# Block L1 of a four-layer decoder: VectorE's order written out, weights rounded behind the clips, both partial sums on one engine, output tiles spread over the batches

## The chip, the core and the metric

The kernel runs on one core of a Trainium2 chip. The metric is the device time of one execution in microseconds. All times of engines below come from one profiled execution, in microseconds from the start of its span unless marked otherwise.

Engines are called as in the profile: PE is TensorE, PEld its weight loads, DVE VectorE, ACT ScalarE, POOL GpSimd, SP the queue that issues most DMAs.

## What is computed

Four layers of cross attention and a feed-forward network (FFN) over 8 batches of 100 tokens of 512 numbers, with a context of 361 positions a batch. The change touches layer L1 alone:

```
# attention: 16 heads of 32, keys and values from the context
q, k, v = proj(layernorm(x)), proj(context), proj(context)
scores = clip(q @ k / sqrt(32), -50, 50); masked positions become -50
probs  = softmax(scores); probs = probs / (sum(probs) + 1e-8)
delta  = clip(residual_scale, 0, 0.3) * (probs @ v @ Wo.T + bo)
x      = x + layernorm(delta) * gamma + beta
# FFN with ternary weights (w1 is 2048 x 512, w2 512 x 2048)
weight_quant(w)     = clip(round(w / mean|w|), -1, 1) * mean|w|
activation_quant(y) = round(y * 127 / max|y|) / (127 / max|y|), by token
h = relu(activation_quant(layernorm(x)) @ weight_quant(w1).T)
x = x + activation_quant(h) @ weight_quant(w2).T
```

## The kernel before

The 800 tokens lie in SBUF as seven tiles of 128 tokens (the last has 32). L1's attention goes batch by batch. Its functions, with the names that appear in the profile:

- `kv_pieces(b)` makes the keys and values of a batch: four key blocks, each four matmul pairs of TensorE and a copy out of PSUM with bias on ScalarE (`kT`, line 1321), and three value blocks, copied out by VectorE (`va`, line 1329). They are handed out in pieces (`k[0]` to `k[3]`, `v[0]` to `v[2]`), to be put between other work of TensorE.
- `weigh(b, c)` handles chunk c of the context positions (128, 128 and 105 of them): 32 small matmuls give the scores of 16 heads (the last eight use the fourth key block), VectorE clips them in two halves (line 1465), ScalarE takes the Exp of each half (line 1467, tile `pT`).
- Between chunks the three `pT` of a batch are added up, tile `added`: the sum of the first two on GpSimd (line 1473), the third added by VectorE (line 1475).
- `gather(b)` sums over positions with a matmul by ones (`l`), multiplies the weights by the values, and scales by the reciprocal (`rl`, lines 1500 to 1504).
- `Ternary` prepares w1 and w2, four blocks of 128 x 2048 each, through two load buffers `v`: `add_up` takes absolute sums on ScalarE (line 1596), `quantise` scales, clips and rounds in two steps on VectorE (lines 1609 and 1610) and a third on ScalarE (line 1611). `park` writes w2's rounded blocks to DRAM. These steps are `fillers`, a list of 18; one is taken in each of the 18 stages (b = 0 to 5, c = 0 to 2).
- `OutputAndFFN` holds the output projection by tile: `product` (matmul), `scaled` (scale, bias, statistics and a Sqrt), `added` (norm, sum into x, statistics of the new x and a Sqrt), then the FFN by tile: `quantise` (norm and rounding of a tile), `turn_y`, `widen`, `round_h`, `turn_h`, `narrow`.

TensorE's order is the order of the program in this part. `held(...)` does the same for an instruction of another engine; those not held are put in place by a scheduler. In `before`, the steps of `Ternary.quantise` and GpSimd's sum are not held. Work waits for its buffers: TensorE's results have four buffers of one PSUM bank (`ps1`) and two of two banks (`ps2`; a `weigh` takes both).

In `before` each stage of the first six batches runs `weigh`, then the pieces and `gather` of the batch before, and last its filler:

```
weigh(b, c)
...                       # pieces of keys and values, gather(b - 1)
if fillers:
    fillers.pop(0)()
```

Batch 6 and 7 follow written out. The output tiles 0 to 3 stand in batch 6, two ahead of its last chunk and two behind it. In the FFN loop (`run`) tile i + 4's `product` and `scaled` stand ahead of `narrow(i - 1)`, its `added` behind it.

Of the kernel before, what the change touches and what calls it, by code (L numbers as in the profile page):

```python
# [59 lines left out]
def decoder_kernel(ctx: ExitStack, tc: tile.TileContext, a: dict, out: bass.AP):  # L60
# [1365 lines left out]
    def clipped_attention(ctxT, begun, st, fillers, begin_ffn):  # L1426

        root = HR  # L1430
        wq, wk, wv, wo, rs, bqk, bv, msc, mbi, kst, kvp, kv = begun
        res = st.enter_context(tc.tile_pool(name="a1", bufs=1))
        qT = project_q(res, wq, bqk[:, 0, :], held=True)
        hst = st.enter_context(ExitStack())
        hp = hst.enter_context(tc.tile_pool(name="a1h", bufs=2))
        beta = hp.tile([128, 4, KD * LQ], F32, name="pT", bufs=4)[:, 0:2, :].rearrange("p g q -> p (g q)")[:, :D]
        nc.sync.dma_start(out=beta, in_=a["a1_beta"].partition_broadcast(128))
        add_row_to_x(beta)
        ffn = begin_ffn(wq, wo, rs)
        ffn.qT = qT  # L1440

        weights = {}
        added = {}

        def weigh(b, c):

            toks = slice(b * LQ, (b + 1) * LQ)
            k0, kn = KCH[c]
            kT = kv[b][0]
            pT = hp.tile([128, 4, KD * LQ], F32, name="pT", bufs=4)  # L1450
            weights.setdefault(b, []).append(pT)
            s = [ps2(), ps2()]
            for j in range(KD):
                for g in range(4):
                    rows = four_heads(g)
                    matmul(
                        s[g // 2][:kn, g % 2, j * LQ : (j + 1) * LQ],
                        lhsT=kT[rows, j, k0 : k0 + kn],
                        rhs=qT[rows, j, toks],
                        start=True,  # L1460
                        stop=True,
                    )
            for i in range(2):
                dst = pT[:kn, 2 * i : 2 * i + 2, :]
                held(nc.vector.tensor_scalar(dst, s[i][:kn, :, : KD * LQ], LIM * root, -LIM * root, ALU.min, ALU.max))  # L1465
                held(
                    nc.scalar.activation(  # L1467
                        dst, dst, AF.Exp, bias=mbi[:kn, b, c : c + 1], scale=msc[:kn, b, c : c + 1]
                    )
                )  # L1470
            if b < NB - 1 and c == 1:
                added[b] = hp.tile([128, 4, KD * LQ], F32, name="added", bufs=1)
                nc.gpsimd.tensor_tensor(added[b], weights[b][0], pT, ALU.add)
            elif b < NB - 1 and c == 2:
                held(nc.vector.tensor_tensor(added[b][:kn], added[b][:kn], pT[:kn], ALU.add))

        def gather(b):

            _, va, _ = kv.pop(b)
            pTs = weights.pop(b)  # L1480
            p, l = ps1(), ps1()
            parts = [(added.pop(b), 128)] if b in added else [(pT, kn) for pT, (_, kn) in zip(pTs, KCH)]
            for i, (pT, kn) in enumerate(parts):
                if i == 2:
                    yield
# [37 lines left out]
        with in_order():  # L1523
            for b in range(NB - 2):
                k, v = pieces(b + 1) if b else (kv[1][2][0::2], kv[1][2][1::2])
                for c in range(3):
                    weigh(b, c)
                    if b == 0:
                        several(*((k[1], k[2]), (v[1], v[2]), (k[3],))[c])
                    elif c == 0:  # L1530
                        several(k[0], k[1])
                        for _ in gather(b - 1):
                            pass
                        several(v[0])
                    elif c == 1:
                        several(v[1], k[2], v[2])
                    else:
                        several(k[3])
                    if fillers:
                        fillers.pop(0)()  # L1540
            assert not fillers
            k, v = pieces(NB - 1)
            weigh(NB - 2, 0)
            several(k[0], k[1])
            for _ in gather(NB - 3):
                pass
            several(k[2])
            weigh(NB - 2, 1)
            several(k[3])
            for t in (0, 1):  # L1550
                ffn.product(t)
                ffn.scaled(t)
            weigh(NB - 2, 2)
            for t in (2, 3):
                ffn.product(t)
                ffn.added(t - 2)
                ffn.scaled(t)
            weigh(NB - 1, 0)
            several(v[0])
            ffn.added(2)  # L1560
            ffn.added(3)
            for _ in gather(NB - 2):
                pass
            several(v[1])
            ffn.quantise(0)
            weigh(NB - 1, 1)
            several(v[2])
            ffn.quantise(1)
            weigh(NB - 1, 2)
            ffn.turn_y(0, nc.vector.tensor_copy)  # L1570
            last = gather(NB - 1)
            next(last)
            ffn.widen(0, (0, 1))
            next(last)
        hst.close()
        kst.close()
        return ffn
# [3 lines left out]
    class Ternary:  # L1581
# [24 lines left out]

        def quantise(self, i, dst):
            w = load_v(self.src[i])
            nc.vector.tensor_scalar(w, w, self.inv, 1.0, ALU.mult, ALU.min)
            nc.vector.tensor_scalar(w, w, -1.0, MAGIC, ALU.max, ALU.add)  # L1610
            nc.scalar.activation(dst, w, AF.Identity, bias=unmagic)  # L1611

        def park(self, i, spare):

# [34 lines left out]
    class OutputAndFFN:  # L1649
# [18 lines left out]
        def scaled(self, t):  # L1668
# [6 lines left out]
                )  # L1675
            )
            self.done[t] = d
            self.statistics(d, *(v[:rows, t, :] for v in self.stats[0:2]))

        def statistics(self, src, mv, rstd):  # L1680
            st = small.tile([128, 6], F32, name="st")[: src.shape[0]]
            held(nc.vector.bn_stats(st, src))
            held(nc.vector.bn_aggr(mv, st))
            held(nc.scalar.activation(rstd, mv[:, 1:2], AF.Sqrt, bias=eps[: src.shape[0]]))

        def added(self, t):

# [3 lines left out]
            held(nc.vector.reciprocal(rstd, rstd))  # L1691
            held(nc.vector.scalar_tensor_tensor(d, d, mv[:, 0:1], self.gamma[:rows, :], ALU.subtract, ALU.mult))
            held(nc.vector.scalar_tensor_tensor(x[:rows, t, :], d, rstd, x[:rows, t, :], ALU.mult, ALU.add))
            self.statistics(x[:, t, :], *(v[:, t, :] for v in self.stats[2:4]))

        def scales(self, amax, step, mean):

# [99 lines left out]
        def run(self, hp):  # L1797

            q2 = self.w2.fetch()
            for i in range(NTT + 1):  # L1800
# [5 lines left out]
                    self.widen(i, (1,))  # L1806
                if i + 1 < NTT:
                    self.turn_y(i + 1)
                if i < NTT:
                    self.round_h(i, hp)  # L1810
                if i + 2 < NTT:
                    self.quantise(i + 2)
                ahead = i + 4 < NTT
                if ahead:
                    self.product(i + 4)
                    self.scaled(i + 4)
                if i:
                    self.narrow(i - 1, q2)
                if ahead:
                    self.added(i + 4)  # L1820

# [900 lines left out]
```

## Time and profile before

| | |
|---|---|
| times of three runs | 1981.69, 1985.65, 1990.58 us |
| median | 1985.65 us |
| the profiled execution | 1981.62 us, its span 1979.8 us |
| mean granted clock of TensorE | 0.978 |
| L1's batches and FFN | from 602 to 909 us of the span |
| TensorE busy in the span | 1868.0 us (94%) |
| VectorE, ScalarE, GpSimd busy | 851.0, 541.7, 273.3 us |

A line of a timeline gives the start, the duration, the engine, the line of the kernel, the operation, the tile written and the tiles read, their shapes, how many instructions were merged, and in brackets how long the engine stood idle before and what released it. f32 matmuls appear as two instructions each. Where two successive instructions overlap in the pipeline, the time from start to start is what one costs.

### The profile page before, as it was taken

The numbers are of one execution on the slowest core, as the hardware profiler recorded it, in microseconds if no ns is written. First come the engines' busy times: TensorE is split into PE (matmuls) and PEld (weight loads), VectorE is DVE, ScalarE is ACT, GpSimd is POOL, SyncE is SP. The second block draws the span as 40 slices with busy tenths as digits, with TensorE's granted clock in tenths as the row PEclk, the third lists the DMA queues.
The fourth block names the chain that finished last, engine by engine and source line by source line (L and its number), as shares of the span: only waits on it lengthen the run. The fifth ranks groups of instructions, "written<-read, shape, count | busy, mean of one in ns | idle before, by whom it ended". The sixth has DMA issues, their size and how long they took to land.

```text
span 1979.8 us, 28538 instructions
## 1 busy us (share of the span) xinstructions
PE 1868.0 (94%) x11992; PEld 1109.6 (56%) x11992; DVE 851.0 (43%) x1577; ACT 541.7 (27%) x1167; POOL 273.3 (14%) x220
## 2 busy tenths in 40 slices
PE   6999999899989989888999998999999999999996
PEld 3676666343355545434555554555445555569994
DVE  4354444445354584884455555111113443432222
ACT  1243323134414453563244443100001111111110
POOL 4200000033033011001000000000001000033553
PEclk8999999999989999899999999999999999999998
DMA  9601000188953260011000001111101000057883
GB/s 272 214 25 33 24 9 22 37 326 248 293 199 102 86 213 22 23 43 53 22 2 1 1 22 43 43 43 43 43 0 59 16 2 1 12 170 231 267 243 73
DMA packets 62957, 177.21 MB, mean 90 GB/s; under 512 B 19079, under 2 KB 27571, under 8 KB 55905
## 3 DMA queue, kind: packets, MB, share of 16 engines
q1 hardware_dynamic: 35234, 134.08, 20.1%
q0 software_dynamic: 22576, 31.96, 6.2%
q10 hardware_dynamic: 5006, 9.22, 1.4%
q8 instruction: 98, 1.61, 0.3%
q14 instruction: 43, 0.34, 0.1%
HBM read 149.25 MB, written 21.65 MB: 86 GB/s over the span
## 4 chain that ended last, share of the span: by engine, by line
PE 60%; DVE 7%; DMA 5%; ACT 5%; issue 2%; POOL 1%; POOLq 0%; SPq 0%; DVEq 0%; ACTq 0%
PE ps L103 57%; PE ps L108 3%; DMA out_x<-o,r_row 3%; ACT sc L1865 1%; DMA v<-in_f_w 1%; ACT pT L1467 1%; DVE va L1329 1%; ACT h L1775 1%; POOL got L1267 1%; DVE sc L1871 1%; ACT hq L1780 1%; DVE amax L1761 1%; DVE pT L1465 1%; DVE nmx L1861 0%; ACT q_f_w L1611 0%
## 5 line engine op out<-in xcount | busy, mean ns | idle before, releaser
L103 PE MATMUL ps<-yT,w 128*128 128x400 f32 x768 | 263.8, 505 | 0.7 <-DVE yT L83 0.7
L103 PE MATMUL ps<-w,ctxT 128*128 128x512 f32 (+1 forms) x576 | 263.1, 600 | 0.0
L103 PE MATMUL ps<-ctxT,w 128*128 128x361 f32 x768 | 251.3, 476 | 0.0
L103 PEld LDWEIGHTS ps<-yT,w 128*128 128x128 f32 x768 | 146.4, 192 | 114.1 <-issue 5.8
L103 PEld LDWEIGHTS ps<-ctxT,w 128*128 128x128 f32 x768 | 142.5, 191 | 90.8 <-issue 16.2
L103 PEld LDWEIGHTS ps<-w,ctxT 128*128 128x128 f32 (+1 forms) x576 | 102.0, 183 | 117.6 <-issue 109.2
L1321 ACT ACTIVATE kT<-ps,bqk 128x361 f32<-128x361 f32 x96 | 53.5, 559 | 213.4 <-PE ps L103 207.7
L103 PE MATMUL ps<-xT,w 128*128 128x152 f32 (+1 forms) x768 | 104.6, 297 | 1.2 <-ACT xT L85 1.2
L103 PEld LDWEIGHTS ps<-xT,w 128*128 128x128 f32 (+1 forms) x768 | 101.1, 184 | 2.5 <-ACT xT L85 1.5
L1329 DVE TENSOR_TENSOR va<-ps,r_a_bv 128x512 f32<-128x512 f32 (+1 forms) x72 | 49.6, 689 | 116.4 <-PE ps L103 116.4
L103 PE MATMUL ps<-w_vo,oc 128*128 128x512 f32 (+1 forms) x224 | 90.5, 598 | 0.0
L952 DVE TENSOR_TENSOR hT<-sg,ps 128x400 f32<-128x400 f32 x36 | 20.6, 571 | 158.3 <-PE ps L103 156.0
L103 PE MATMUL ps<-w,qT 128*128 128x512 f32 (+1 forms) x184 | 83.4, 619 | 5.0 <-DVE qT L2166 4.7
L233 DVE TENSOR_TENSOR x<-x,ps 128x512 f32<-128x512 f32 (+1 forms) x51 | 34.9, 685 | 121.5 <-PE ps L103 121.4
L1865 ACT ACTIVATE sc<-ps,nmx 100x361 f32<-100x361 f32 x128 | 70.2, 561 | 50.0 <-DVE nmx L1861 50.0
L2178 POOL IOTA counts<- 128x2 f32 x2 | 0.2, 134 | 552.3 <-PE ps L103 552.3
L108 PEld LDWEIGHTS ps<-ident,sc 100*128 100x128 f32 (+1 forms) x512 | 52.8, 148 | 41.0 <-issue 26.1
L2491 POOL DMA_INDIRECT out_x<-o,r_row x32 | 59.4, 1856 | 89.1 <-DMA out_x<-o,r_row 34.8
L666 ACT ACTIVATE sc<-sc,nmx 100x128 f32<-100x128 f32 x128 | 49.8, 390 | 79.4 <-DVE nmx L663 78.6
L108 PE MATMUL ps<-ident,sc 100*128 100x100 f32 (+1 forms) x512 | 61.3, 255 | 6.3 <-DVE va L1329 3.9
L1467 ACT ACTIVATE pT<-pT,mbi,msc 128x800 f32<-128x800 f32 (+1 forms) x48 | 47.9, 1045 | 54.0 <-DVE pT L1465 53.4
L2093 DVE TENSOR_SCALAR kp<-ps,mask 128x512 f32<-128x512 f32 (+1 forms) x48 | 33.8, 747 | 65.2 <-PE ps L103 65.2
(399 smaller groups left out, 2831.2 us busy)
## 6 DMA issues: line engine op xcount, KB each, us to landing
w<-in_f_gu SPq DMA_DIRECT2D x32, 704.0 KB, 6.3
wd<-in_f_dn SPq DMA_DIRECT2D x32, 512.0 KB, 6.2
v<-in_f_w SPq DMA_DIRECT2D x16, 1024.0 KB, 5.5
v<-in_f_dn SPq DMA_DIRECT2D x16, 768.0 KB, 7.5
w<-in_a_w SPq DMA_DIRECT2D x11, 1024.0 KB, 4.9
w<-in_f_gu SPq DMA_DIRECT2D x9, 1024.0 KB, 4.8
gu<-in_f_gu SPq DMA_DIRECT2D x8, 1024.0 KB, 16.6
cx<-in_ctxT SPq DMA_DIRECT2D x8, 722.0 KB, 17.9
```

Of the source, the lines that this page charges most:

```text
L103: ins = nc.tensor.matmul(dst, **args)
L108: ins = nc.tensor.transpose(dst, src, unit)
L233: nc.vector.tensor_tensor(x[:rows, t, :], x[:rows, t, :], p[:rows, :], ALU.add)
L666: nc.scalar.activation(sc[:, g, :], sc[:, g, :], AF.Exp, bias=nmx[:, g : g + 1], accum_out=l[:, g : g + 1])
L952: nc.vector.tensor_tensor(dst, sg[:rows, :n], pu[:rows, :n], ALU.mult)
L1267: nc.gpsimd.indirect_dma_start(out=got[t][:rows, i, :], out_offset=None, in_=back, in_offset=bass.IndirectOffsetOnAxis(ap=where_i[:rows, t ...
L1321: ins = nc.scalar.activation(kT[:, m, :], p[:, :LK], AF.Identity, bias=bk[:, m : m + 1])
L1329: ins = nc.vector.tensor_tensor(va[:kn, c, :, 0:HD], p[:kn, :].rearrange("p (h d) -> p h d", d=HD), bv[:kn, :].rearrange("p (h d) -> p h d ...
L1467: nc.scalar.activation(dst, dst, AF.Exp, bias=mbi[:kn, b, c : c + 1], scale=msc[:kn, b, c : c + 1])
L1865: nc.scalar.activation(sc[:, h, :], s[i][:LQ, g, :LK], AF.Exp, bias=nmx[:, g : g + 1], accum_out=l[:, h : h + 1])
L2093: nc.vector.tensor_scalar(kps[b][:kn, c, 2 * i : 2 * i + 2, :, :].rearrange("p g j f -> p g (j f)"), s[i][:kn, :, : KD * F], 0.0, mask[:kn ...
L2491: nc.gpsimd.indirect_dma_start(out=flat, out_offset=bass.IndirectOffsetOnAxis(ap=r_row[:, e, h : h + 1], axis=0), in_=o[:, h, :], in_offse ...
```

## The change

In each stage of the first six batches the filler stands right behind `weigh`, ahead of the pieces, and the three steps of `quantise` are held, so that VectorE's two steps come right behind the clips. The first sum of a batch (`add(b, 1)`) moves from GpSimd to VectorE and stands behind the pieces of chunk 1; the second (`add(b, 2)`) stands behind the clips of the next batch's first chunk. Output tile 0 moves to the end of chunk 1 of the fifth batch (b = 4), tile 1 to that of the sixth (b = 5), with `added(0)`. Tiles 2 and 3 stay in batch 6. The Sqrt of `added` becomes a step of its own, `rooted`, placed later; in the FFN loop `rooted(i + 2)` stands ahead of `round_h(i)` and `added(i + 3)` behind `quantise(i + 2)`.

```diff
-            if b < NB - 1 and c == 1:
+
+        def add(b, c):
+
+            kn = KCH[c][1]
+            if c == 1:
                 added[b] = hp.tile([128, 4, KD * LQ], F32, name="added", bufs=1)
-                nc.gpsimd.tensor_tensor(added[b], weights[b][0], pT, ALU.add)
-            elif b < NB - 1 and c == 2:
-                held(nc.vector.tensor_tensor(added[b][:kn], added[b][:kn], pT[:kn], ALU.add))
+            other = weights[b][0] if c == 1 else added[b]
+            held(nc.vector.tensor_tensor(added[b][:kn], other[:kn], weights[b][c][:kn], ALU.add))
...
                     weigh(b, c)
+                    if b and c == 0:
+                        add(b - 1, 2)
+                    fillers.pop(0)()
...
-                    if fillers:
-                        fillers.pop(0)()
+                    if c == 1:
+                        add(b, 1)
+                        if b == NB - 4:
+                            ffn.product(0)
+                            ffn.scaled(0)
+                        elif b == NB - 3:
+                            ffn.product(1)
+                            ffn.added(0)
+                            ffn.scaled(1)
             weigh(NB - 2, 0)
+            add(NB - 3, 2)
...
-            for t in (0, 1):
-                ffn.product(t)
-                ffn.scaled(t)
+            ffn.product(2)
+            ffn.rooted(0)
+            ffn.added(1)
+            ffn.scaled(2)
+            add(NB - 2, 1)
             weigh(NB - 2, 2)
-            for t in (2, 3):
-                ffn.product(t)
-                ffn.added(t - 2)
-                ffn.scaled(t)
+            ffn.product(3)
+            ffn.rooted(1)
+            ffn.added(2)
+            ffn.scaled(3)
             weigh(NB - 1, 0)
+            add(NB - 2, 2)
+            ffn.quantise(0)
             several(v[0])
-            ffn.added(2)
-            ffn.added(3)
...
-            nc.vector.tensor_scalar(w, w, self.inv, 1.0, ALU.mult, ALU.min)
-            nc.vector.tensor_scalar(w, w, -1.0, MAGIC, ALU.max, ALU.add)
-            nc.scalar.activation(dst, w, AF.Identity, bias=unmagic)
+            held(nc.vector.tensor_scalar(w, w, self.inv, 1.0, ALU.mult, ALU.min))
+            held(nc.vector.tensor_scalar(w, w, -1.0, MAGIC, ALU.max, ALU.add))
+            held(nc.scalar.activation(dst, w, AF.Identity, bias=unmagic))
...
                     self.turn_y(i + 1)
+                if i + 2 < NTT:
+                    self.rooted(i + 2)
                 if i < NTT:
                     self.round_h(i, hp)
                 if i + 2 < NTT:
                     self.quantise(i + 2)
-                ahead = i + 4 < NTT
-                if ahead:
+                if i + 3 < NTT:
+                    self.added(i + 3)
+                if i + 4 < NTT:
                     self.product(i + 4)
                     self.scaled(i + 4)
                 if i:
                     self.narrow(i - 1, q2)
-                if ahead:
-                    self.added(i + 4)
```

More of the change, by code (lines that the diff above doesn't have):

```diff
@@ L1564, in clipped_attention @@
             several(v[1])
-            ffn.quantise(0)
             weigh(NB - 1, 1)
+            ffn.quantise(1)
             several(v[2])
-            ffn.quantise(1)
             weigh(NB - 1, 2)
+            last = gather(NB - 1)
             ffn.turn_y(0, nc.vector.tensor_copy)
-            last = gather(NB - 1)
             next(last)
@@ L1677, in scaled, with statistics @@
             self.done[t] = d
-            self.statistics(d, *(v[:rows, t, :] for v in self.stats[0:2]))
-        def statistics(self, src, mv, rstd):
+            self.statistics(d, self.stats[0][:rows, t, :])
+            self.root(*(v[:rows, t, :] for v in self.stats[0:2]))
+        def statistics(self, src, mv):
             st = small.tile([128, 6], F32, name="st")[: src.shape[0]]
@@ L1683, in statistics, with root, rooted @@
             held(nc.vector.bn_aggr(mv, st))
-            held(nc.scalar.activation(rstd, mv[:, 1:2], AF.Sqrt, bias=eps[: src.shape[0]]))
+        def root(self, mv, std):
+            held(nc.scalar.activation(std, mv[:, 1:2], AF.Sqrt, bias=eps[: mv.shape[0]]))
+        def rooted(self, t):
+            self.root(*(v[:, t, :] for v in self.stats[2:4]))
         def added(self, t):
@@ L1693, in added @@
             held(nc.vector.scalar_tensor_tensor(x[:rows, t, :], d, rstd, x[:rows, t, :], ALU.mult, ALU.add))
-            self.statistics(x[:, t, :], *(v[:, t, :] for v in self.stats[2:4]))
+            self.statistics(x[:, t, :], self.stats[2][:, t, :])
         def scales(self, amax, step, mean):
```

## The prediction, made before the changed kernel was run

> **What bounds the kernel.** I read the page first, then the timelines of TensorE, VectorE and ScalarE from 575 to 910 us, which is L1.
>
> ```profile
> PE 1868.0 (94%) x11992; PEld 1109.6 (56%) x11992; DVE 851.0 (43%) x1577; ACT 541.7 (27%) x1167; POOL 273.3 (14%) x220
> 643.58 1.00 PE L103 MATMUL ps<-qT,kT 32*105 32x100 f32 x32
> 644.51 2.70 PE L103 MATMUL ps<-ctxT,w 128*128 128x361 f32 x8
> 647.14 1.54 PE L103 MATMUL ps<-qT,kT 32*128 32x100 f32 x32
> ...
> 735.65 2.50 PE L103 MATMUL ps<-qT,kT 32*128 32x100 f32 x24 [5.83 <-DVE pT L1465]
> 739.16 0.77 PE L103 MATMUL ps<-qT,kT 32*128 32x100 f32 x8 [1.01 <-ACT kT L1321]
> 739.86 7.16 PE L103 MATMUL ps<-ctxT,w 128*128 128x361 f32 x16
> ...
> 821.80 0.67 PE L103 MATMUL ps<-qT,kT 32*105 32x100 f32 x4 [7.61 <-DVE pT L1465]
> ...
> 872.33 3.63 PE L103 MATMUL ps<-v,hqT 128*128 128x512 bf16 x16 [2.87 <-ACT hqT L1722]
> ```
>
> TensorE is the bound. The change leaves its matmuls as they are, so I count only what PE loses in L1: idle time, and matmuls at a lower clock. Batches are b = 0 to 7, chunks c = 0 to 2.
>
> ```profile
> 643.69 0.69 DVE L1329 TENSOR_TENSOR va<-ps,r_a_bv 105x512 f32<-105x512 f32 x1 [5.17 <-PE ps L103]
> 644.61 1.89 DVE L1465 TENSOR_SCALAR pT<-ps 105x800 f32<-105x800 f32 x2 [0.23 <-PE ps L103]
> 645.70 2.00 ACT L1467 ACTIVATE pT<-pT,mbi,msc 105x800 f32<-105x800 f32 x2 [2.99 <-DVE pT L1465]
> 647.60 0.54 ACT L1321 ACTIVATE kT<-ps,bqk 128x361 f32<-128x361 f32 x1
> 648.05 1.90 ACT L1596 ACTIVATE q_f_w<-v 128x2048 bf16<-128x2048 f32 x1
> 694.09 3.58 POOL L1473 TENSOR_TENSOR added<-pT 128x1600 f32<-128x1600 f32 x1 [25.99 <-ACT pT L1467]
> 694.46 4.30 DVE L1610 TENSOR_SCALAR v<-v 128x2048 f32<-128x2048 f32 x1
> ```
>
> The first five lines are the turn from one batch to the next. PE's scores of c = 2 end at 644.51, the next batch's scores begin at 647.14, and their last eight matmuls need the fourth key block: clip, two Exps, the key's copy, ready at 648.15. PE loses 0.4 (1.54 against 1.15 elsewhere). The last two lines: a rounding of weights that takes 1.22 alone takes 4.30 beside POOL's sum.
>
> **Lost before.** Four such turns, 1.6. At 703.63, 0.9. At 735, where weights' rounding stands before the clips: 5.83 + 1.01 idle and 4.1 of slow matmuls (2.50, 0.70 and 7.09 from start to start, for 0.81, 0.27 and 5.07): 11.0. At 821, where four output tiles stand before the clips: 7.61 + 0.23 and 3.9 slow, likewise: 11.8. The FFN's ten waits (0.38, 1.25, 0.46, 2.87, 0.65, 1.25, 1.17, 0.99, 2.99, 0.25): 12.3. Sum 37.6.
>
> **Part 1: both sums on VectorE.** Seven POOL sums of 3.57 go, and with them the 3.1 that one cost the rounding. Seven of 1.75 (796.37 to 798.12) come. The first sum of a batch now stands after the last value copy and ahead of the clips of c = 2. With 0 at the end of the value matmuls: copy to 0.7, sum to 2.5, clips to 3.4 and 4.35. The scores were ready at 1.0, so the clips are 1.4 late.
>
> **Part 2: the filler right behind the clips, rounding on ScalarE held.** In the instruction order of the changed kernel, ScalarE has the filler of c = 2 between the Exps and the fourth key copy; before it was the other way round. PE waits for that copy. Undisturbed, PE would reach it at 4.3 (scores 0.93, key 2.6, first scores 0.8). Now (0.1 for a hand-over, as 644.51 to 644.61; Exps of 0.95):
> - b = 0, 1: Exps to 5.4, absolute sum 2.0, copy 0.5, PE at 8.0: 3.7 lost each.
> - b = 2, no filler: PE at 6.0: 1.7.
> - b = 3: rounding on VectorE 2.45 (732.15 to 734.61) to 6.8, on ScalarE 6.9 to 8.85, copy, PE at 9.45: 5.1.
> - b = 4 also has an output tile: PE is due at 7.85 (product 3.5). Its scaling and statistics (1.6, from 3.6) push the clips to 7.05, rounding to 9.5, ScalarE to 11.55, PE at 12.15: 4.3.
> - b = 5 adds `added` (2.4): clips to 8.35, rounding to 10.8, PE at 13.45: 5.6.
> Turns: 24.1. In c = 0 of b = 4 and 5 the rounding delays the first key's copy to 8.7 after the scores, and its PSUM buffer is the value matmul's, due at 7.95: 0.8 each, 1.7. In c = 1 the rounding's 2.45 fits the 5.17 that VectorE stood before 643.69. SP's order does not change; a weight block's load is issued behind the rounding two blocks before and lands 5.6 to 7.9 later; two stages take at least 14 us (c = 1 to the next c = 0), of which that rounding uses 5, so no load is late. If one were, VectorE's line would stand still with the clips behind it, as at 735.
>
> **Part 3: output tiles spread.** The 11.8 goes. Left: the turn to b = 7, 1.0; from the third product's end VectorE has scaling 1.6, sum 1.75, clips 1.85, `added` 2.4, scaling 1.6, clips 1.85, sum 1.75 = 12.9, where PE has 10.0 until it needs that sum: 3.0; before the first wide matmul clips and a copy, 1.8. Together 5.8.
> The Sqrt of a tile now goes out with its tile, which needs an Exp table again (1.28, its Exp 0.01 later). In b = 4 the Exps end at 8.8, where ScalarE waits for VectorE until 9.6; the same 0.8 in b = 5. So it costs nothing, and what it exceeds 0.8 by otherwise. The Trainium skill (ScalarE: Activation LUTs, What ACT_TABLE_LOAD costs) gives 2.66 us a switch, which speaks against this part: by it the two turns would be 0.6 longer each and the sum 1.1 higher; the trace shows no such second half.
>
> **Part 4: roots apart from norms.** In the FFN a tile with a product took 12.3 (854.13 to 866.45) though VectorE has 10.7 of work in it; it stood 1.6 for the Sqrt. With the Sqrt issued a turn ahead, PE's own 11.7 is the bound, and the waits of 1.25, 0.46, 2.87, 0.65 and 0.38 go. A Sqrt ahead of the first rounding brings one of 1.2. 12.3 becomes 7.9.
>
> **Clock.** After: 24.1 + 1.7 + 5.8 + 7.9 = 39.5, against 37.6: 1.9 more, before the clock. Three turns leave PE idle 4.1 in one piece (b = 3, 4, 5), two 2.8, one wait 3.0. What a gap costs:
>
> ```profile
> 1223.72 1.37 PE L108 MATMUL ps<-ident,y 128*128 128x128 f32 x8 [3.00 <-DVE y L200]
> 1224.00:1227.00 3.00, 2.91 (x11) 1.50 (x10) 2.00 (x6) 0.96 (x3) 0.00 (x0) 0.71 0.00 0
> 1227.00:1230.00 3.00, 3.00 (x6) 1.20 (x5) 0.34 (x1) 0.00 (x0) 0.00 (x0) 0.72 0.00 0
> 1955.00:1960.00 5.00, 4.65 (x7) 2.03 (x8) 0.57 (x2) 0.00 (x0) 3.60 (x2) 0.66 0.18 17
> 872.00:874.00 2.00, 1.67 (x8) 0.80 (x9) 2.00 (x5) 0.76 (x2) 0.00 (x0) 1.00 0.93 393
> ```
>
> (Columns: stretch, its length, busy time and instructions of the five engines, granted clock, DMA share, GB/s.) After 3.00 idle the clock was 0.71 and 0.72 for six us, 1.7 lost; after 3.76 (ahead of 1955), 0.66, 1.7 lost; after 2.87, nothing; after 5.83, 4.1. So a gap of 4.1 costs 1.7 to 4.1; I take 2.5, as 3.76 is the nearest: 7.5, less the 1.7 of value waits that a slower PE no longer sees. The three shorter ones lie between nothing and 1.7: half, 2.5. Clock: 8.3. The Trainium skill (TensorE: Matmul & The Clock Gate, Part 1) has the clock halved only after a whole free-running window of some 3.4 us idle, by which the gap of 3.00 should have cost nothing; an estimate by it has a fifth of the 4.1 gaps drop, the sum then near 3; the rows decide.
>
> **Sum.** 1.9 + 8.3 = 10.2; my hand-overs of 0.1 are generous by some 1 over L1, so 9 us. The profiled execution took 1981.62 (span 1979.8), and would take 1990.6. The median of the three runs, 1985.65, is 4.0 above it; 1985.65 + 9 is about 1994.
>
> **Rivals.**
> - Clock at every gap: all six drop for as long as at 735 (4.1 each, 24.6 in place of 8.3). For it: the 2.99 at 907.92 was followed by seven slow microseconds. Against it: 872. It decides once more than four gaps cost 3 or more. 1994 + 16 = 2010. Chance 0.10.
> - The turns are cheap: the key's copy isn't what PE waits for, the first scores run late anyway, and a turn costs 1 in place of 3.7 to 5.6. For it: PE lost only 0.4 there. Against it: 739.16, released by exactly this copy. Price: 24.1 becomes 6, and 8.3 of clock goes: 26 less, 1968. Chance 0.10.
> - Losses only change places: the sum of 39.5 is right and the clock stays up, 1985.65 + 2 = 1988. For it: the skipped drop at 872. Chance 0.12.
>
> **How the numbers follow.** The forecast (0.68) spans 1987 to 2003: clock prices at their ends, hand-overs, and the spread of the runs (4 either way). A measurement of this kernel tells apart about 0.5%, 9.9 us, so its centre is just inside. Of its 0.68 I put 0.36 within and 0.32 above; with the rivals: faster 0.10, same 0.48, slower 0.42. The range takes in the third rival and most of the first, and leaves out the second: 1980 to 2008.
>
> **What would show it.** Right: PE's idle at each turn from b = 0 to 5 released by the kT copy, 2.8 (b = 0, 1) and about 4 (b = 3 to 5), with the filler between Exps and copy on ScalarE; no wait over 5 us at 735 or 821; FFN tiles some 11.7 apart; the clock under 0.8 after the 4 us gaps. Wrong: turns under 1 us, VectorE waiting for a weight load, or batches 1 and 2 as long as before (27.2).

## The result and the profile after

| | before | after |
|---|---|---|
| median of 15 runs | 1985.65 us | 1997.91 us |
| lowest, highest | 1978.79, 1990.58 | 1990.66, 2006.97 |
| profiled execution, its span | 1981.62, 1979.8 | 2006.55, 2004.6 |
| L1, from the first scores to the last narrow product | 306.6 | 319.4 |

The ratio after to before is 1.0067, with a 95% interval of 1.0049 to 1.0084: slower by 13.3 us (9.7 to 16.7). The forecast was 1994, in a range of 1980 to 2008. L1's length is read from the two traces: 908.77 - 602.17 and 926.50 - 607.13, so 12.8 longer. The profiled execution of after lies 8.6 above its median and that of before 4.0 below its own, so these two differ by more than the medians do. The other 12 us of their difference lie ahead of L1 (5.0) and behind it, where the change moves nothing; I read L1 alone.

The totals of the profile of after show little: TensorE is busy for 10.0 more than before with the same 11992 matmuls, which is slow matmuls and not more work (in the whole span, so not in L1 alone).

```profile
PE 1878.0 (94%) x11992; PEld 1115.8 (56%) x11992; DVE 859.9 (43%) x1584; ACT 545.5 (27%) x1169; POOL 247.1 (12%) x213
```

TensorE's timeline of after. The lines ending in x8 with a kT in brackets are the last eight score matmuls of a batch's first chunk. The key blocks are the lines of x16.

```profile
629.27 0.77 PE L103 MATMUL ps<-qT,kT 32*128 32x100 f32 x8 [2.56 <-ACT kT L1321]
629.97 8.03 PE L103 MATMUL ps<-ctxT,w 128*128 128x361 f32 x16
...
662.93 0.60 PE L103 MATMUL ps<-qT,kT 32*128 32x100 f32 x8 [2.62 <-ACT kT L1321]
663.46 6.66 PE L103 MATMUL ps<-ctxT,w 128*128 128x361 f32 x16
...
691.52 0.91 PE L103 MATMUL ps<-qT,kT 32*128 32x100 f32 x20 [0.36 <-DVE pT L1465]
693.16 0.48 PE L103 MATMUL ps<-qT,kT 32*128 32x100 f32 x8 [0.73 <-ACT kT L1321]
...
694.18 6.64 PE L103 MATMUL ps<-ctxT,w 128*128 128x361 f32 x16
...
727.17 0.77 PE L103 MATMUL ps<-qT,kT 32*128 32x100 f32 x8 [4.03 <-ACT kT L1321]
727.86 6.88 PE L103 MATMUL ps<-ctxT,w 128*128 128x361 f32 x16
...
763.81 0.76 PE L103 MATMUL ps<-qT,kT 32*128 32x100 f32 x8 [4.07 <-ACT kT L1321]
764.50 7.33 PE L103 MATMUL ps<-ctxT,w 128*128 128x361 f32 x16
...
802.23 0.76 PE L103 MATMUL ps<-qT,kT 32*128 32x100 f32 x8 [4.07 <-ACT kT L1321]
802.92 6.90 PE L103 MATMUL ps<-ctxT,w 128*128 128x361 f32 x16
...
835.30 0.88 PE L103 MATMUL ps<-added,ones 128*32 128x400 f32 x8 [2.77 <-DVE added L1478]
```

All six turns wait for the fourth key copy; both jams of before (TensorE's waits of 5.83 and 7.61 for clips, at 735 and 821) are gone. Taken from the start of the scores of c = 2 to the start of the next key block, less the 4.64 of the matmuls in between (0.93, 2.63 and 1.08), the turns lose 3.9, 3.8, 1.8, 5.4, 4.7 and 6.0: 25.6. In the turn 2 to 3 a product by ones (0.61) is left out. What was not expected stands in the x16 lines: the key block behind every turn is slow, also behind 693.16, where no gap is over 0.73.

ScalarE's timeline in the turn 3 to 4 shows the chain: two Exps, the rounding's third step, and only then the key's copy.

```profile
721.38 2.00 ACT L1467 ACTIVATE pT<-pT,mbi,msc 105x800 f32<-105x800 f32 x2 [6.09 <-DVE pT L1465]
724.67 2.00 ACT L1627 ACTIVATE q_f_w<-v,unmagic 128x2048 bf16<-128x2048 f32 x1 [1.29 <-DVE v L1626]
726.57 0.54 ACT L1321 ACTIVATE kT<-ps,bqk 128x361 f32<-128x361 f32 x1
```

The granted clock (the share of its full speed that TensorE got) over three of the six key blocks of after (stretch, length, busy time of PE, PEld, DVE, ACT and POOL, clock, DMA share, GB/s):

```profile
629.97:638.00 8.03, 8.03 (x24) 4.55 (x24) 3.78 (x4) 4.46 (x5) 0.00 (x0) 0.63 0.53 192
694.18:700.80 6.62, 6.62 (x21) 3.77 (x24) 3.44 (x7) 2.56 (x3) 0.00 (x0) 0.76 0.01 2
764.50:771.80 7.30, 7.30 (x24) 4.13 (x23) 6.04 (x5) 3.03 (x3) 0.00 (x0) 0.69 0.37 139
```

From start to start the six key blocks take 7.96, 6.58, 6.58, 6.81, 7.26 and 6.82, in place of 5.07: 2.9, 1.5, 1.5, 1.7, 2.2 and 1.8 more, 11.6 in all.

### The profile page after: what moved, and what is told of

Same layout as the page of the kernel before. It is cut to its first block, busy times and chain, and to the rows that moved or that the text cites. A ratio compares the mean times of both kernels' runs of the same rounds, so it can differ in the third digit from the quotient of the medians.

```text
span 2004.6 us, 28525 instructions
## 1 busy us (share of the span) xinstructions
PE 1878.0 (94%) x11992; PEld 1115.8 (56%) x11992; DVE 859.9 (43%) x1584; ACT 545.5 (27%) x1169; POOL 247.1 (12%) x213
## 4 chain that ended last, share of the span: by engine, by line
PE 54%; DVE 6%; ACT 4%; DMA 3%; issue 1%; POOL 0%; POOLq 0%; SPq 0%; DVEq 0%; ACTq 0%
PE ps L103 52%; PE ps L108 3%; DMA out_x<-o,r_row 2%; ACT sc L1889 1%; DMA xs<-normal,r_tok 1%; DVE va L1329 1%; DVE pT L1465 1%; DVE sc L1895 1%; DVE nmx L1885 0%; ACT h L1798 0%; DVE added L1478 0%; ACT hq L1803 0%; ACT q_f_w L1627 0%; ACT pT L1467 0%; DVE y L200 0%
## 5 line engine op out<-in xcount | busy, mean ns | idle before, releaser
L103 PE MATMUL ps<-ctxT,w 128*128 128x361 f32 x768 | 260.9, 490 | 0.0
L103 PEld LDWEIGHTS ps<-ctxT,w 128*128 128x128 f32 x768 | 147.6, 198 | 95.6 <-issue 25.2
L233 DVE TENSOR_TENSOR x<-x,ps 128x512 f32<-128x512 f32 (+1 forms) x51 | 34.9, 685 | 120.5 <-PE ps L103 120.3
```

The costliest lines, as they stand in the source:

```text
L103: ins = nc.tensor.matmul(dst, **args)
L233: nc.vector.tensor_tensor(x[:rows, t, :], x[:rows, t, :], p[:rows, :], ALU.add)
```

## The experiments

Theory: ScalarE's order at the turn (filler ahead of the key's copy), with the first sum's delay of the clips, makes TensorE wait, and the waits pull its clock down. Rivals: VectorE's load is the limit; the sum costs nothing; the slow blocks are something else than the clock; and the FFN's or the tiles' gains do not exist. The kernels in one table. Each ratio is to runs of before taken with it; L1 is read as above, from one trace each:

| kernel | median us | ratio to before (95%) | L1 |
|---|---|---|---|
| after | 1997.91 | 1.0067 (1.0049 to 1.0084) | 319.4 |
| key copy ahead of the filler | 1985.60 | 1.0007 (0.9990 to 1.0025) | 305.6 |
| value block in the turn | 1968.12 | 0.9907 (0.9886 to 0.9929) | 284.5 |
| first sum on GpSimd | 1990.31 | 1.0014 (0.9997 to 1.0031) | 309.7 |
| gaps filled | 1989.77 | 1.0014 (0.9993 to 1.0036) | 308.3 |
| before, FFN part | 1978.21 | 0.9956 (0.9938 to 0.9973) | 299.0 |
| before, tiles spread | 1987.33 | 0.9996 (0.9978 to 1.0015) | 306.6 |
| before, FFN part and value block in the turn | 1977.02 | 0.9947 (0.9925 to 0.9970) | 296.8 |
| value block in the turn, more cover | 1961.24 | 0.9865 (0.9843 to 0.9887) | 280.3 |
| the same, first sum on GpSimd | 1956.52 | 0.9861 (0.9834 to 0.9888) | 278.6 |

One more, with the scores four times, had one execution (1993.0) and is read from its trace.

### Key copy ahead of the filler

```diff
-                    fillers.pop(0)()
+                    if c < 2:
+                        fillers.pop(0)()
...
                         several(k[3])
+                    if c == 2:
+                        fillers.pop(0)()
```

> The changed kernel (1997.9 us) with one line moved: in c = 2 the fourth key block is issued ahead of the filler, so that ScalarE copies the key before it does its absolute sum or rounding. Theory A (ScalarE's order decides the turn, the first sum on VectorE adds its 1.4): the six turns lose 1.7, 1.7, 1.7, 1.7, about 0.7 and 2.0 in place of 3.9, 3.8, 1.8, 5.4, 4.7 and 6.0, so 16 us less; no wait for the key's copy above 2. The clock then splits it in two. A1, only gaps of 2.5 us or more pull the clock down: the 11.6 us that the slow key blocks cost go too, and the time is near 1970. A2, the clock falls where some 3.4 us hold nothing but small score matmuls and short gaps, as after the turn 2 to 3 of the changed kernel (gaps of 0.36 and 0.73 only): the key blocks behind most turns stay at 6.5 in place of 5.07, and the time is near 1980. Rival B (the key's copy is late because VectorE is late, not because of the filler): the waits stay at 2.6 and 4.0, the time at 1998.

TensorE's timeline, turns 0 to 1, 1 to 2 and 4 to 5:

```profile
622.30 0.48 PE L103 MATMUL ps<-qT,kT 32*128 32x100 f32 x8 [0.67 <-ACT kT L1321]
622.71 5.13 PE L103 MATMUL ps<-ctxT,w 128*128 128x361 f32 x16
...
650.89 0.48 PE L103 MATMUL ps<-qT,kT 32*128 32x100 f32 x8 [0.73 <-ACT kT L1321]
651.30 6.80 PE L103 MATMUL ps<-ctxT,w 128*128 128x361 f32 x16
...
746.10 0.48 PE L103 MATMUL ps<-qT,kT 32*128 32x100 f32 x8 [2.01 <-ACT kT L1321]
```

The turns lose 1.7, 1.8, 1.8, 1.8, 2.3 and 3.9, together 13.4 (9.5 expected; the last two came higher, with a tile's scaling and a table load ahead of the clips). So ScalarE's order was worth 12.2 of the 25.6, where 16 were expected. Rival B falls. Of the clock A2 holds: five of the six key blocks stay slow, 9.4 us in place of 11.6. The first turn loses 1.74 and its block runs at 5.13, the second loses 1.80 and its block takes 6.80. 12.2 + 2.2 = 14.4; L1 is 13.8 shorter, the median 12.3.

### Value block in the turn

```diff
-                        several(*((k[1], k[2]), (v[1], v[2]), (k[3],))[c])
+                        several(*((k[1], k[2]), (v[1], k[3]), (v[2],))[c])
...
-                        several(v[1], k[2], v[2])
+                        several(v[1], k[2], k[3])
                     else:
-                        several(k[3])
+                        several(v[2])
```

> The changed kernel with two blocks of TensorE swapped in the first six batches: the fourth key block moves into c = 1 and the third value block into c = 2, so that behind the scores of c = 2 stands a block that no score matmul waits for, and the first sum no longer stands behind that value copy. Filler and sums stay where the change put them. Theory A (the turn costs what it does because TensorE waits for the fourth key copy): no wait for a key copy at the turns, 25.6 us of turn losses become under 3, and the stretch without a dense block shrinks to about 1.2 us, so that the 11.6 of slow clock go as well: about 1962, below the kernel before (1985.65). Rival B (VectorE is the bound at the turn: clips, sum, rounding): the waits come back as waits for clips or for a value's PSUM buffer, and the time stays above 1985. Rival C (the clock falls for another reason than what stands at the turn): the waits go, the key blocks stay at 6.6 to 7.9, and the time is near 1974.

TensorE's timeline, the turn 1 to 2 and two places of c = 0:

```profile
645.92 3.68 PE L103 MATMUL ps<-w,ctxT 128*105 128x512 f32 x8
649.53 1.15 PE L103 MATMUL ps<-qT,kT 32*128 32x100 f32 x32
650.61 5.13 PE L103 MATMUL ps<-ctxT,w 128*128 128x361 f32 x16
...
713.48 3.70 PE L103 MATMUL ps<-w,ctxT 128*128 128x512 f32 x8 [0.87 <-ACT kT L1321]
...
745.33 3.70 PE L103 MATMUL ps<-w,ctxT 128*128 128x512 f32 x8 [1.57 <-ACT kT L1321]
```

The turns have no gap, and the six key blocks take 5.11 to 5.14. L1 is 34.9 shorter than in the changed kernel and the median 29.8; expected were 36. Rivals B and C fall: once TensorE has other work at the turn, the filler and the sums where the change put them no longer hold it up there. The swap also takes the first sum from behind the third value copy, so this run does not part the two. The waits of 0.87 and 1.57, which Rival B named, are new but small; they are the value's PSUM buffer of the prediction, discussed below.

### First sum on GpSimd

```diff
-            held(nc.vector.tensor_tensor(added[b][:kn], other[:kn], weights[b][c][:kn], ALU.add))
+            if c == 1:
+                nc.gpsimd.tensor_tensor(added[b], other, weights[b][c], ALU.add)
+            else:
+                held(nc.vector.tensor_tensor(added[b][:kn], other[:kn], weights[b][c][:kn], ALU.add))
```

> The changed kernel with the first sum of each batch (weights of c = 0 plus c = 1) back on GpSimd; everything else as changed. Theory A (on VectorE it delays the clips of c = 2 by 1.4): each turn's wait for the key copy falls by 1.4, to 1.2 in b = 0 and 1, to nothing in b = 2 and to 2.7 in b = 3 to 5; 8 us less, and 1.5 more where the clock stays up after the turn 2 to 3: 1989. If the clock also stays up after the turns whose gap falls to 1.2, 1985. Rival B (the sum fills a hole of VectorE and costs nothing, the filler on ScalarE is all): waits as before this edit, 1998. Rival C (GpSimd's sum slows the roundings beside it from 1.25 to over 4, as at 694.46 of the kernel before): roundings of 4, and the time at 1998 or above.

TensorE's timeline, turns 2 to 3, 3 to 4 and 4 to 5:

```profile
687.17 1.54 PE L103 MATMUL ps<-qT,kT 32*128 32x100 f32 x32
...
719.16 0.77 PE L103 MATMUL ps<-qT,kT 32*128 32x100 f32 x8 [3.43 <-ACT kT L1321]
...
756.62 0.77 PE L103 MATMUL ps<-qT,kT 32*128 32x100 f32 x8 [4.07 <-ACT kT L1321]
```

The turns lose 2.2, 2.3, 0.4, 4.0, 4.7 and 4.7: 18.2, which is 7.4 less, in five turns by 1.3 to 1.7 and not at all in batch 4. There VectorE waits for the output tile's product ahead of the clips, and the sum fits into that wait (in the changed kernel it ends at 754.28, and VectorE then stands 1.01). The key block behind the turn 2 to 3 is back at 5.11. The wait of 2.77 for the second sum falls to 1.83. So Theory A holds (1989 expected, 1990.3 measured), without batch 4. Rival C falls: the roundings keep their 1.28 and 1.23.

### Scores four times

```diff
-            for j in range(KD):
+            for j in [j for _ in range(4 if c == 1 and 1 <= b <= 5 else 1) for j in range(KD)]:
```

> The kernel before, with the 32 score matmuls of c = 1 issued four times over in batches 1 to 5 (same values written again), so that TensorE has 4.3 us of 32-row score matmuls in one piece and no idle time; nothing else changes. It measures the clock by itself. Theory I (the clock goes by idle time): each of the five stretches costs its 3.25, 16 us in all, the value block behind it runs at its 3.6 to 3.7 and the granted clock stays 1.00. Theory II (the clock goes by how little of the array works, small matmuls counting nearly as nothing): the value blocks behind them take 4.5 or more, the clock there is 0.5 to 0.8, and the five cost 16 plus 1.5 to 2.5 each, 24 to 28 us.

TensorE's timeline at the first of the five places, and the granted clock over the block behind it:

```profile
632.47 3.83 PE L103 MATMUL ps<-qT,kT 32*128 32x100 f32 x128
636.23 3.70 PE L103 MATMUL ps<-w,ctxT 128*128 128x512 f32 x8
```

```profile
636.23:639.90 3.67, 3.67 (x13) 1.76 (x10) 1.89 (x2) 2.00 (x2) 0.40 (x1) 1.00 0.02 4
```

The 128 matmuls took 3.76 from start to start, so the three repeats cost 2.7 and not 3.25 (a score matmul takes 0.03). At all five places the block behind takes 3.70 and the clock is 1.00. So 3.8 us of nothing but small matmuls, without gaps, leave the clock up. Theory II falls. This rests on the clock and the block lengths of one trace; one time says nothing on the price.

### Gaps filled

```diff
-            for j in range(KD):
+            for j in [j for _ in range({1: 4, 2: 4, 3: 3, 4: 6, 5: 6, 6: 6}.get(b, 1) if c == 0 else 1) for j in range(KD - 1)] + [KD - 1]:
```

> The changed kernel (1997.9 us), where TensorE, at the turns of batches 0 to 5, repeats the first 24 score matmuls of the next batch (the same values written again) two to five times while it waits for the fourth key copy: 0.82 us of work a time, 2.5 us in the turns into batches 1 and 2, 1.6 into 3, 4.1 into 4, 5 and 6. It removes no wait: VectorE and ScalarE do what they did, and the key's copy comes when it came. Theory A (the clock goes by how long TensorE stands idle in some 3.4 us, and the 11.6 us of slow key blocks are the price of the idleness alone): the key blocks behind the turns come down from 6.6 to 8.0 to 5.1, the granted clock stays at 1.00 there, and the time falls by 8 to 12 us, to 1986 to 1990, although work was added. Rival B (the clock falls because the dense blocks stop, small matmuls counting as nothing): key blocks stay at 6.6 or more, 1998. Rival C (the slow key blocks are not the clock but ScalarE's or VectorE's late hand-overs, or the weight loads beside them): no change, 1998, with the clock at 1.00.

TensorE's timeline at the turn 1 to 2 and in c = 0 of batch 4, and the granted clock over two key blocks:

```profile
656.14 2.92 PE L103 MATMUL ps<-qT,kT 32*128 32x100 f32 x92 [0.36 <-DVE pT L1465]
659.67 0.48 PE L103 MATMUL ps<-qT,kT 32*128 32x100 f32 x8 [0.61 <-ACT kT L1321]
660.08 5.13 PE L103 MATMUL ps<-ctxT,w 128*128 128x361 f32 x16
...
730.08 3.70 PE L103 MATMUL ps<-w,ctxT 128*128 128x512 f32 x8 [0.71 <-ACT kT L1321]
```

```profile
660.08:665.20 5.12, 5.12 (x24) 3.01 (x24) 3.62 (x3) 3.93 (x5) 0.00 (x0) 1.00 0.63 208
756.75:761.90 5.15, 5.15 (x24) 3.04 (x24) 5.01 (x5) 2.00 (x2) 0.00 (x0) 1.00 0.57 204
```

With 552 matmuls more, L1 is 11.1 shorter than in the changed kernel, and the median 8.1. The key's copies still end each turn, but all six key blocks are back at 5.1 and the clock at 1.00. This shows the clock's share by itself: the edit changes only what TensorE does while it waits, so the 11.6 us of slow key blocks hang on its idleness in the turn. Two waits of 0.71 and 0.76 appear in c = 0 of batches 4 and 5; the slow key block had hidden them.

### Before, FFN part

```diff
                 ffn.added(t - 2)
+                ffn.rooted(t - 2)
...
             weigh(NB - 1, 0)
             several(v[0])
             ffn.added(2)
-            ffn.added(3)
...
-            self.statistics(x[:, t, :], *(v[:, t, :] for v in self.stats[2:4]))
+            self.statistics(x[:, t, :], self.stats[2][:, t, :])
...
+                if i + 2 < NTT:
+                    self.rooted(i + 2)
...
+                if i + 3 < NTT:
+                    self.added(i + 3)
...
-                if ahead:
-                    self.added(i + 4)
```

> The kernel before with the FFN part of the change alone: a tile's second root apart from its norm and a turn ahead in the FFN's loop, and the sum of tile i + 3 taken ahead of the product of tile i + 4. L1's loop over batches is as before. Theory A (prediction: TensorE's own 11.7 becomes the bound of a tile with a product): the ten FFN waits of 12.3 become about 8.8, as they are in the changed kernel, so 3.5 to 4.4 less than 1986: 1982. Rival (the waits belong to VectorE's load and only change places): waits of 12 and 1986.

TensorE's timeline, the former stall at 821:

```profile
822.59 0.45 PE L103 MATMUL ps<-qT,kT 32*105 32x100 f32 x4 [4.31 <-DVE pT L1465]
823.49 1.74 PE L103 MATMUL ps<-qT,kT 32*105 32x100 f32 x28 [0.45 <-DVE pT L1465]
```

The FFN's waits fall from 12.3 to 8.9, by 3.4 as expected. The time fell by 8.7 (5.4 to 12.3) and L1 by 7.6, more than that, because tile 3's `added` has left batch 7 for the FFN's loop: the stall of 7.61 and 0.23 becomes 4.31 and 0.45, 3.1 less. Theory A holds, and half of what the prediction gave to the spread tiles (11.8 less 5.8) belongs to this edit.

### Before, tiles spread

```diff
+                    if c == 1 and b == NB - 4:
+                        ffn.product(0)
+                        ffn.scaled(0)
+                    elif c == 1 and b == NB - 3:
+                        ffn.product(1)
+                        ffn.added(0)
+                        ffn.scaled(1)
...
-            for t in (0, 1):
-                ffn.product(t)
-                ffn.scaled(t)
+            ffn.product(2)
+            ffn.added(1)
+            ffn.scaled(2)
             weigh(NB - 2, 2)
-            for t in (2, 3):
-                ffn.product(t)
-                ffn.added(t - 2)
-                ffn.scaled(t)
+            ffn.product(3)
+            ffn.added(2)
+            ffn.scaled(3)
             weigh(NB - 1, 0)
             several(v[0])
-            ffn.added(2)
             ffn.added(3)
```

> The kernel before with the third part alone: output tiles 0 and 1 in the fifth and sixth batch, 2 and 3 one to a stage of batch 6, roots with their norms as before, GpSimd's first sums and the order of fillers as before. Theory A: the stall at 821 (7.61 and 0.23 idle, 3.9 of slow matmuls, 11.8 in all) goes, and about 4 to 5 of it come back as waits for a sum, an yqT and the turn to batch 7; in the turns of batches 4 and 5 a tile's scaling, statistics and table load lie ahead of the clips and cost TensorE 2 and 4.4. Net 1 to 4 less than 1986: 1984. Rival (the two turns also lose the clock, as every turn with over 2 us of idle did in the changed kernel): plus 2 each, 1988.

TensorE's timeline, and ScalarE's at the first of these turns:

```profile
739.93 2.50 PE L103 MATMUL ps<-qT,kT 32*128 32x100 f32 x24 [3.67 <-DVE pT L1465]
744.89 0.77 PE L103 MATMUL ps<-qT,kT 32*128 32x100 f32 x8 [2.47 <-ACT kT L1321]
...
779.77 0.48 PE L103 MATMUL ps<-qT,kT 32*128 32x100 f32 x8 [2.00 <-ACT kT L1321]
780.18 6.82 PE L103 MATMUL ps<-ctxT,w 128*128 128x361 f32 x16
...
825.42 0.67 PE L103 MATMUL ps<-qT,kT 32*105 32x100 f32 x4 [5.30 <-DVE pT L1465]
```

```profile
739.49 1.28 ACT L1689 ACT_TABLE_LOAD   x1
740.79 0.29 ACT L1689 ACTIVATE s<-s,eps 128x1 f32<-128x1 f32 x1
741.10 1.28 ACT L1467 ACT_TABLE_LOAD   x1
742.40 2.00 ACT L1467 ACTIVATE pT<-pT,mbi,msc 105x800 f32<-105x800 f32 x2
```

No change, in time or in L1: 7.61 at 821 becomes 5.30 only, where Theory A had it go, and the turn 5 to 6, free before, has a wait of 2.00 and a slow block, as the rival says. The times, 1984 and 1988 expected and 1987.3 measured, lie too close to decide: the interval is 3.7 either way. ScalarE needs 2.9 from the one table load to the Exp behind the other, the Sqrt included.

### Before, FFN part and value block in the turn

The edits of two runs above (the FFN part, and the value block in the turn), on the kernel before.

> The kernel before with the FFN part (1978.2 us measured) and, besides, the swap that puts the third value block into c = 2 and the fourth key block into c = 1. VectorE's order in L1 is not written out: roundings stand where the scheduler puts them, the first sum is on GpSimd, four output tiles stand in batch 6. It asks whether the written order of the change is worth anything once the turn has its cover. Theory A (it is: rounding ahead of clips and four tiles in a row cost two jams that a swap of two blocks does not remove): waits of 3 us and more for clips stay in batch 4 and ahead of 821, the clock falls behind them, and the time is 1972 to 1978, some 10 to 16 above the version with the written order (1961.2). Rival (cover is all that matters): under 1966.

TensorE's timeline, the two former stalls:

```profile
738.10 2.93 PE L103 MATMUL ps<-qT,kT 32*128 32x100 f32 x32 [5.91 <-DVE pT L1465]
...
819.25 0.43 PE L103 MATMUL ps<-qT,kT 32*105 32x100 f32 x4 [4.31 <-DVE pT L1465]
```

Both jams are still there, and the time lies in Theory A's range. The swap gains 1.2 here, too little to be told from the scatter of the runs, and 29.8 in the changed kernel. With the swap the changed kernel is 8.9 faster than this one (1968.1 against 1977.0): the written order and the spread tiles are worth that, once the turn is covered.

### More cover: the version that beats both

```diff
                         several(k[0], k[1])
+                        fillers.pop(0)()
                         for _ in gather(b - 1):
...
-            several(v[0])
+            several(v[0], v[1])
             for _ in gather(NB - 2):
                 pass
-            several(v[1])
...
             several(v[2])
+            ffn.turn_y(0, nc.vector.tensor_copy)
             weigh(NB - 1, 2)
             last = gather(NB - 1)
-            ffn.turn_y(0, nc.vector.tensor_copy)
```

The value block in the turn is kept, and in the stages c = 0 of b = 1 to 5 the filler stands where it is shown and no longer behind `weigh`.

> The version meant to beat both. It is the kernel with the value block in the turn (1968.1 us measured) and three more moves for the waits that its trace has left: in c = 0 the filler behind the two key blocks, so that ScalarE copies the keys ahead of a rounding (waits of 0.87 and 1.57); the value block of c = 1 of the last batch ahead of the gathering of batch 6 (a wait of 2.77 for the sum); the first tile's transposes ahead of the last scores (1.09). Theory A (each of these waits is TensorE's own loss): 6.3 less, about 1962. Rival (they are taken up by the next wait, VectorE having some 8 us of work per c = 0 and 1 in batches 3 to 5): 1968.

TensorE's timeline, the one wait that came in another's place:

```profile
807.39 3.61 PE L103 MATMUL ps<-q_f_w,yqT 128*128 128x512 bf16 x16 [1.43 <-DVE pT L1465]
```

1961.2, by the medians 24.4 below before and 36.7 below after. In TensorE's timeline the waits of 0.87, 1.57 and 2.77 are gone; that of 1.09 for the yqT has become the one of 1.43 for a clip. Theory A holds for three of the four waits, the rival for the fourth. L1 is 4.2 shorter, the median 6.9.

> The best version so far (1961.2 us) with part 1 of the change half undone: the first sum of each batch on GpSimd. Theory A (with a value block in the turn nobody waits for that sum, so its 1.8 us on VectorE cost and gain nothing): 1961, within 2. Rival (GpSimd's sum slows the roundings beside it, from 1.25 to 4 in batches 3 to 5, and clips come late behind them): waits of 1 to 3 for clips in batches 3 to 5, 1964 to 1968.

Only the first sum differs from the version above, by the same edit as before. VectorE's and GpSimd's timelines in c = 1 of batch 5:

```profile
747.87 1.23 DVE L1630 TENSOR_SCALAR v<-v 128x2048 f32<-128x2048 f32 x1
...
749.68 3.40 DVE L1719 SCALAR_TENSOR_TENSOR w<-w,s 128x512 f32<-128x512 f32 x1
```

```profile
747.91 4.63 POOL L1479 TENSOR_TENSOR added<-pT 128x1600 f32<-128x1600 f32 x1 [26.29 <-ACT pT L1467]
```

The ratios of the two versions, 0.9861 and 0.9865, cannot be told apart. Roundings stay at 1.2 to 1.3; a norm step takes 3.40 in place of 0.73 once. TensorE waits for neither. When the turn is covered, Part 1 of the change has no gain and no cost that these runs can tell.

## Why the prediction was right or wrong

The direction of the centre was right, its size too small: 9 us were forecast, L1 shows 12.8 and the ratio 13.3. 0.67% lies just past the 0.5% that the prediction took for what can be told apart (the interval begins at 0.49%), so it was the case given 0.42 and not the likelier one of 0.48.

- **Turns: right.** 3.7, 3.7, 1.7, 5.1, 4.3 and 5.6 were forecast (24.1); 3.9, 3.8, 1.8, 5.4, 4.7 and 6.0 came (25.6). Part of each excess is the last eight score matmuls, which from start to start took 0.41 (693.16) to 0.70 (629.27) behind the wait, in place of 0.27. The cause was right too: moving the key's copy ahead of the filler gave back 12.2 of the 16 expected, moving the sum off VectorE 7.4 of the 8.4 that six times 1.4 make. The sum's 1.4 was right for five turns and wrong for batch 4.
- **Hand-overs "generous by some 1": wrong.** No turn came shorter.
- **Value waits of 0.8 each: right, and hidden.** They do not appear in the changed kernel. With the gaps filled they are 0.71 and 0.76, with the value block in the turn 0.87 and 1.57. The prediction took them off again as what a slower TensorE does not see, and that is what happened.
- **Tiles spread: 5.8 forecast, 4.7 came** (0.8 at the turn to batch 7, 2.77 and 1.09). The seven terms ahead of the wait for the sum add up to 12.8 and not to 12.9, so the working gives 2.8, and 2.77 came. The stall at 821 went, but, as the runs with one part show, half through tile 3's `added` moving into the FFN. By themselves the spread tiles gained nothing that the runs can tell.
- **Table loads: right.** In batch 4 of the changed kernel the Exps behind the second load end at 761.25 and VectorE's rounding, which ScalarE needs next, at 761.23: the load costs nothing. The Trainium skill (ScalarE: Activation LUTs, What ACT_TABLE_LOAD costs) counts a drain into each switch, 2.66 in all; in the four lines of ScalarE above, from the kernel with the tiles spread, a switch is 1.28 and the next instruction starts 0.02 behind it.
- **FFN: 7.9 forecast, 8.8 came** (1.25, 1.17, 0.94, 1.25, 0.99, 3.00, 0.24); the 0.94, for ScalarE's `h`, was not in the working. Tiles with a product are 11.5 and 11.7 apart, as said.
- **Clock: the term with the wrong reasons; 10.0 forecast, 11.6 came.** Losses without it are 25.6 + 4.7 + 8.8 = 39.1, with it 50.7, which is 13.1 above the 37.6 of before. The working has 37.8 without it, as its 39.5 hold the 1.7 of value waits that it takes off again. So of the 4 us by which 9 fell short, 1.6 are the clock, 1.3 the other terms and 1.0 the hand-overs. The 10.0 were 2.5 for each of three gaps of 4, which cost 1.7, 2.2 and 1.8 (5.7, not 7.5), and 2.5 for three shorter gaps, two of them turns. The turns 0 to 1, 1 to 2 and 2 to 3 cost 2.9, 1.5 and 1.5 (5.9), the last of them not on the list at all, and the third short gap on it, the wait for the sum (2.77), cost nothing in this trace. That 10.0 lies so near 11.6 is in part luck: one half was 1.8 too high, the other 3.4 too low. The error was to price the longest single gap of a turn by single gaps elsewhere: in a turn the gap lies in a stretch in which TensorE already works little. And one row, "after 2.87, nothing", was taken for an end of the price; the same wait, in the runs with the tiles spread and with the scores four times, was followed by a block of 5.31 in place of 3.63, so it costs nothing or 1.7.
- **Rivals.** "Clock at every gap" expected six drops, and six came, but behind all six turns and not behind the wait for the sum, and at the wrong price: 1.5 to 2.9 each and not 4.1. "The turns are cheap" is false: 25.6 against its 6. "Losses only change places" had the right sum, 39 against 37.6, but the clock did not stay up.

## What to carry over

When an order on one engine is rewritten, look for the one copy on another engine that the bottleneck needs next, and put that copy first, or put work for the bottleneck that does not need it in between. Here swapping two blocks of TensorE was worth 30 us in the changed kernel, and 1.2 in the kernel before with the FFN part, where the copy already stood first. A stretch of waits can cost TensorE twice, once as idle time and once as the slow block behind it; in the changed kernel the second price was close to half the first.

## What the runs showed of the hardware

The clock fell here without one long gap. Turns of five kernels without their jams, by what TensorE lost in them (idle time and slow matmuls between the scores of c = 2 and the next key block) and the key block behind, 5.13 at full clock:

| kernel | lost at the turns: key block behind |
|---|---|
| before | 0.3: 5.13; 0.4: 5.13 (three turns); 1.1: 5.13 |
| key copy ahead of the filler | 1.74: 5.13; 1.79: 6.79 and 6.82; 1.80: 6.80; 2.3: 6.82; 3.9: 7.83 |
| first sum on GpSimd | 0.4: 5.11; 2.2 and 2.3: 6.82; 4.0 to 4.7: 7.70 to 7.76 |
| after | 1.80: 6.64; 3.8 to 6.0: 6.66 to 8.03 |
| tiles spread | 1.1: 5.13; 2.3: 6.82 |

Up to 1.74 lost there was no drop, from 1.79 on there was one each time. At 1.80 the stretch between the two key blocks (648.42 to 651.30) is 2.9 long, of which the score matmuls fill 1.1, and the granted clock over the block behind it is 0.75. Filled with small matmuls such turns cost nothing, nor did 3.8 of small matmuls without a gap.

The same single gap cost in one trace and not in another. The wait of 2.77 for the sum cost nothing in after (835.30), with the value block in the turn and with the gaps filled, but 1.4 with the key copy ahead of the filler (815.68). The FFN's 2.87 cost nothing in before (872.33), but 1.7 with the tiles spread and with the scores four times. Some 3.0 cost in every trace, at the end of L1: the FFN's last two waits (2.99 and 0.25 in before, 3.00 and 0.24 in after, with 0.6 of small matmuls between them) stand ahead of a block of 6.52 in before (granted clock 0.50 and 0.58) and of 5.04 in after (0.70), where the same block for 128 tokens takes 3.63, and it takes 4.88 to 6.52 in all twelve traces. That drop lies behind the end of L1 as read here. A measure of how long TensorE has worked over a stretch of a few us, begun now earlier and now later, would fit these; that is argued and not shown. Whether the step between 1.74 and 1.79 is a threshold or chance is open, and gaps that cost in one trace and not in another speak for chance. The Trainium skill (TensorE: Matmul & The Clock Gate, Part 1) gives an idle window of some 3.4 us, free-running, as the condition; here the clock fell in stretches of 2.9 that were more than a third full, with no gap over 0.73, so the runs decide against that condition in this case.

Between GpSimd and VectorE, whichever started first kept its time in the two places shown. In before the sum that started first took 3.58 and the rounding beside it 4.30 (1.22 alone); in the last version the rounding that started first took 1.23 and the sum 4.63, and then a norm step of VectorE, with two tensors in SBUF, took 3.40 in place of 0.73, while the value copy between them, with one tensor in PSUM, kept its 0.68.
